# A two-layer graph network on one core: the second layer's first product as seven products of combined quarters

## The chip, the cores and the metric

The kernel runs on one core of a Trainium2 chip. Times are device microseconds of one execution; three runs of the kernel before gave 2491.35, 2492.53 and 2493.94 us, and the profile comes from one further execution. TensorE (PE) multiplies matrices into PSUM; VectorE (DVE), ScalarE (ACT) and GpSimd (POOL) do the elementwise work; SyncE (SP) and POOL issue the transfers. Each engine takes its instructions in the order in which they were written for it.

## The reference

There are 16 graphs of 1024 nodes with 256 channels, in float32. Two layers are added to a residual `x`:

```python
h = jnp.maximum(_layernorm(x, axis=-1), 0.0)
x = x + _L0_gnn_ref(h, L0_gnn_para, adj, L0_gnn_kv_w)      # attention, 4 heads
h = jnp.maximum(_layernorm(x, axis=-1), 0.0)
x = x + _L1_gnn_ref(h, adj, W1, b1, g1, be1, W2, b2, g2, be2)
```

The second layer sums over neighbours and then has two linear maps with batch normalisations:

```python
agg = jnp.einsum('nm,bmd->bnd', A_hat, features)
x = agg.reshape(-1, d)
h = jax.nn.relu(_batchnorm(x @ W1.T + b1, g1, be1))
out = h @ W2.T + b2
out = _batchnorm(out, g2, be2)
```

The case concerns `x @ W1.T + b1`, from 256 to 512 channels, for every node of every graph. The batch normalisation after it needs statistics over all 16 graphs, so its result is written to memory, and the rest of the layer runs when all graphs are done.

## The kernel before, in words

**The stages.** A prologue prepares the neighbour matrix and the first graphs. Then one long loop, `attention`, goes through the graphs. A graph has four units (two pairs of heads, two halves of the nodes), a unit has four steps. Each step issues two score tiles `sc` (L934), two exponentials `p` on ACT (L942), the sums of these on DVE (`acc`, L963 and L966), and the values `o` of the step before (L977). When a unit ends, its sums are folded (L1012, L1013) and added up on PE (`sums`, L1026), and its output goes out and back through memory, is scaled (L1075) and added to `x` (L1083). After the loop, `second` does the last product, the batch normalisations and the output.

**Between the steps** the loop advances a generator, `background(b)`. It weaves three things: for graph b-1, the residual's normalisation (`normed`), the sums over neighbours (`aggregate`) and then the product with W1 (`hidden`); for graph b+2, the preparation of its keys, values and queries (`prepare`): its normalisation, the weighing of the adjacency matrix (`w`, L485 and L493 on ACT, L472 on DVE), squares of its features that are sent through memory to be transposed (`sq`, L412), keys and queries. Every piece yields its estimated PE time, and the loop advances the generator up to a share of `total` that is due at the step (L1109 to L1112). So the order on each engine is written out by the program when it is built; nothing is decided at run time. `soon(...)` puts a small DVE action off to the next piece.

**Sums over neighbours.** `aggregate` is already made of seven products of combined quarters. `made` is one PSUM bank (tile `pa`), and each product is followed by one or two DVE sums out of PSUM into `at`, the result (two tiles, halves of the nodes). A scaling by `dbc` (L706) follows when a quarter is complete.

**The product with W1.** `hidden(b)` makes eight tiles `py` of 128 x 512, one for each half `g` of the nodes and each 128 of the 512 channels, each from two contractions of 128 (L171, the line of the helper that records all such matmuls). ACT adds the bias while it copies a tile to `y` (L773), POOL sends `y` to memory (L774), and DVE takes its statistics (L777). All tiles `pa`, `py`, `sums`, and those of keys, values and queries share the pool `ps_mm` of three PSUM banks, in turn. A matmul into a bank waits until the tile that was there has been read.

**The residual.** `x` of a graph is loaded once into a pool of three places; it serves graph b's first normalisation, then takes the outputs of the attention, is saved (`x_d`, L788) and normalised again. `load_x(b + 3)` follows at the end of `normed(b)`.

The last graph is apart: in `background(15)` its own normalisation, sums over neighbours and product follow those of graph 14 (L1110), and the first products of the last stage are woven in.

Of the kernel before, what the change touches and what calls it, by code (L numbers as in the profile page):

```python
# [10 lines left out]
F32 = mybir.dt.float32  # L11
AF = mybir.ActivationFunctionType
ALU = mybir.AluOpType
# [10 lines left out]
def gnn_two_layers_kernel(  # L24
# [34 lines left out]
    vec = const.tile([P, 18], F32, name="vec")  # L59
    nc.sync.dma_start(out=vec, in_=vecs)  # L60
    b1, g1, be1 = (vec[:, i * HC : (i + 1) * HC] for i in range(3))
    b2, g2, be2 = (vec[:, 3 * HC + i * CC : 3 * HC + (i + 1) * CC] for i in range(3))
    stats1 = const.tile([P, HC, B * NH, 6], F32, name="stats1")
    mv1 = const.tile([P, HC, 2], F32, name="mv1")
# [32 lines left out]
    def layers(shifted):  # L97
# [13 lines left out]
        py = st.enter_context(tc.tile_pool(name=f"py_{kind}", bufs=4))  # L111
# [5 lines left out]
        ps_o = st.enter_context(tc.tile_pool(name=f"ps_o_{kind}", bufs=1, space=PSUM))  # L117
        ps_mm = st.enter_context(tc.tile_pool(name=f"ps_mm_{kind}", bufs=3, space=PSUM))

        xs, hs, hts, ats, qs, ks, vs = {}, {}, {}, {}, {}, {}, {}  # L120
        invs = {}
        csums, cbcs, weighted, weighers = {}, {}, {}, {}
        s1s = {}
        complete = set()

# [2 lines left out]
        def soon(action):  # L128

            queue.append(action)  # L130
# [33 lines left out]
        def bank(name):  # L164
            return ps_mm.tile([P, FB], F32, tag="mm", name=name)
# [4 lines left out]
                r = slice(e * HW, (e + 1) * HW)  # L170
                nc.tensor.matmul(dst[r], left[:, r], right, start=start, stop=stop)  # L171

        def load_x(b):
            xs[b] = p3.tile([P, NT, C], F32, tag="x", name=f"x_{b}")
            parts = 4 if b == 0 else 2
            for part in range(parts):
                t = slice(part * NT // parts, (part + 1) * NT // parts)
                nc.sync.dma_start(
                    out=xs[b][:, t], in_=x[b].rearrange("(t p) c -> p t c", p=P)[:, t]
                )  # L180

        def load_adj(q, th, name):
# [61 lines left out]
        def graph():  # L244
# [21 lines left out]
            for u in range(2 * HT):  # L266
# [20 lines left out]
                nc.gpsimd.dma_start(out=dst[:, 6], in_=one)  # L287
                yield 0.0

        def load_later():  # L290
            later["w1"] = big.tile([P, CC, H1], F32, tag="w1", name="w1")
            nc.sync.dma_start(out=later["w1"], in_=w1_t.rearrange("(k p) j -> p k j", p=P))
            later["dbc"] = const.tile([P, N], F32, tag="dbc", name=f"dbc_{kind}")
            nc.sync.dma_start(out=dinv_d.rearrange("(t p) -> p t", p=P), in_=dinv)
            nc.sync.dma_start(
                out=later["dbc"], in_=dinv_d.rearrange("(o n) -> o n", o=1).to_broadcast([P, N])
            )

        class Norm:
# [2 lines left out]

            def __init__(self, b, first):
                tag = "a" if first else "b"
                self.src = xs[b]
# [376 lines left out]
        def aggregate(b):  # L682


            pieces = []
            order = (0, 2, 5, 1, 4, 6, 3)

            def load(upto):
                while len(pieces) <= min(upto, 7 * NP // 2 - 1):
                    i, th = divmod(len(pieces), NP // 2)  # L690
                    i = order[i]
                    a = p8.tile([P, TH, FB], F32, tag="w", name=f"aht_{b}_{i}_{th}")
                    nc.sync.dma_start(out=a, in_=aht_d[i, th])
                    pieces.append(a)

            load(4)
            yield 0.0
            a11, a12, a21, a22 = quarters("b", b)
            at = ats[b] = [
                p3.tile([P, CC, FB], F32, tag="ht", name=f"at_{b}_{g}") for g in range(NH)  # L700
            ]
            c11, c12, c21, c22 = (at[g][:, c, :] for c in (0, 1) for g in (0, 1))
            add, sub = nc.vector.tensor_add, nc.vector.tensor_sub

            def scale(c, g):
                nc.vector.tensor_mul(c, c, later["dbc"][:, g * FB : (g + 1) * FB])  # L706

            def first(m):
                nc.scalar.copy(c12, m)
                sub(a11, s1s["b", b], a11)  # L710

            def second(m):
                add(c11, m, c12)
                sub(a12, a12, a11)
                soon(lambda: scale(c11, 0))

            def fifth(m):
                add(c22, m, c21)
                add(c12, m, c12)
                soon(lambda: scale(c22, 1))  # L720

            def sixth(m):
                add(c21, m, c21)
                soon(lambda: scale(c21, 0))

            def seventh(m):
                add(c12, m, c12)
                scale(c12, 1)

            for i, (left, after) in enumerate(  # L730
                (
                    (a11, first),
                    (a12, second),
                    (a11, lambda m: add(c12, m, c12)),
                    (a21, lambda m: add(c21, m, c12)),
                    (None, fifth),
                    (a22, sixth),
                    (a12, seventh),
                )
            ):  # L740
                made = bank(f"pa_{b}_{i}")
                left = left or s1s["b", b]
                for th in range(NP // 2):
                    n = i * NP // 2 + th
                    load(n + 5)
                    for j in range(TH):
                        t = th * TH + j
                        product(
                            made, left[:, t, :], pieces[n][:, j, :], t == 0, t == NT // 2 - 1
                        )  # L750
                    if th == NP // 2 - 1:
                        after(made)
                    elif i == 0:
                        combine("b", b, nc.vector)
                    yield 1.71
# [34 lines left out]
        def normed(b):  # L790
            while (b, NH - 1) not in complete:
                yield 0.1
            keep(b)
            yield from Norm(b, False).all()
            if b + 3 < B:
                load_x(b + 3)

        def normed_last():

# [12 lines left out]
        def prepare(b, products):  # L812


            w = weighers[b]
            yield from islice(products, 1)
            if b == 2:
                for k in range(CC):
                    yield from weave(islice(products, 3), (0, islice(w, AHEAD // 3)))
                    yield TOP  # L820
                    transposed(b, (k,))
                    yield 1.0
                yield from products
                return
            squares(b)
            yield from weave(islice(products, 3), (0, islice(w, AHEAD // 2)))
            gathered(b, 0)
            yield from weave(islice(products, 1), (0, islice(w, 1)))
            gathered(b, 1)
            yield from weave(islice(products, 2), (0, islice(w, AHEAD // 2 - 1)))  # L830
            yield from products

        endings, turns = [], []
# [1 line left out]
        def background(b):  # L835

            if b == 0:
# [13 lines left out]
                yield from islice(products, 2)  # L851
                yield from prepare(2, products)
                return
            before = hidden(b - 1)
            gather = aggregate(b - 1)
            if b + 1 < B:
# [236 lines left out]
        def attention():  # L1093
# [7 lines left out]
            for s in range(len(steps) + 2):  # L1101
                if s < len(steps):
                    unit, g = steps[s]
                    b = unit.at[0]
                    if s % per_graph == 0:
# [1 line left out]
                        top = False  # L1107
                        bg, done = background(b), 0.0
                        total = (37.6 if b > 0 else 41.0) * (b + 1 < B) + 24.0 * (b > 0) + 6.0 * (b == 0)  # L1109
                        total += 13.7 * (0 < b < B - 2) + 27.4 * (b == B - 1) + 3.0 * (b == 0)  # L1110

                        total -= 10.3 * (b == B - 1)  # L1112
                    made = scores(*unit.at, g)
# [15 lines left out]
                if before is not None:  # L1129
                    (last, g_last), prs = before  # L1130
                    last.values(g_last, prs)
                    if g_last == NG - 1:
# [29 lines left out]
        with st:  # L1162
# [22 lines left out]
            else:  # L1185
# [24 lines left out]
                load_x(1)  # L1210
                load_x(2)
                run(weave(plain_queries(0), (0, weighers[0]), (5, Norm(1, True).all())))
                attention()
                attn.close()
                turns.append(second(kind))
# [340 lines left out]
```

## Time and profile before

| | us |
|---|---|
| median of three runs | 2492.53 |
| profiled execution | 2492.9 |
| its span | 2491.1 |
| PE busy | 2437.8 (98%) |
| DVE busy | 1880.2 (75%) |
| ACT busy | 1401.8 (56%) |
| POOL busy | 428.0 (17%) |
| matmuls of the product with W1 (1024) | 228.2 |
| matmuls of the sums over neighbours, `pa<-aht,h_b` (1536) | 347.3 |
| scores (4096 matmuls) and values (2048) | 499.5 and 494.5 |

A row of the groups names the source line, the engine, the operation, the tile written and the tiles read, their shapes and the number of instructions; then the busy time and the mean duration in ns; then the idle time of the engine just before these instructions and what ended most of it. A row of the waits has the engine, the tile and line that waited, the one that released it, the total in us, how often, and the longest. A row of the timeline has the start in us, the duration, and the instructions, neighbours of one kind taken together. Matmuls overlap, so the distance from one start to the next says what an instruction costs, and not its duration.

### The profile page before, as it was taken

Reading aid. Unit: us, or ns where it says so; the run is one execution under the profiler, and the core shown is the slowest. Engines: PE = TensorE matmul, PEld = TensorE weight load, DVE = VectorE, ACT = ScalarE, POOL = GpSimd, SP = SyncE. Lnnn points to the kernel's source line nnn. Section 1 sums busy time; section 2 is a strip of 40 time slices with the busy share of each in tenths; the row PEclk is TensorE's granted clock in tenths of the full one; section 3 lists DMA queues with packets and bytes.
Section 4 is the critical chain, followed back from the end, with each engine's and each line's share of the span. In section 5 each row is a group of like instructions: output and inputs, shape, how many; then the busy total and the mean of one; then the engine's idle time right before and its main releaser. Section 6 shows DMA issues by size and latency. Waiting matters only on the chain. (4 is left out here: it accounts for less than half of the span.)

```text
span 2491.1 us, 35563 instructions
## 1 busy us (share of the span) xinstructions
PE 2437.8 (98%) x13403; PEld 842.0 (34%) x13403; DVE 1880.2 (75%) x2919; ACT 1401.8 (56%) x1926; POOL 428.0 (17%) x527
## 2 busy tenths in 40 slices
PE   9999999999999999999999999999999999999995
PEld 4333333333333333333333333333333332334444
DVE  5668787877778787878787787868787876766775
ACT  7775564647474746556464747465564634335544
POOL 1540101010101001010101010110101001036652
PEclk9999999999999999999999999999999999999997
DMA  4754535354544544352635445544536335355459
GB/s 149 238 172 170 172 114 200 98 201 130 194 148 174 168 163 161 125 200 86 214 121 186 141 174 169 178 152 151 171 113 204 103 140 169 123 215 220 189 198 374
DMA packets 187909, 421.42 MB, mean 169 GB/s; under 512 B 21832, under 2 KB 81744, under 8 KB 181968
## 3 DMA queue, kind: packets, MB, share of 16 engines
q1 hardware_dynamic: 158560, 311.56, 37.6%
q0 software_dynamic: 29168, 107.50, 11.6%
q8 instruction: 108, 1.77, 0.3%
q14 instruction: 73, 0.60, 0.1%
HBM read 315.63 MB, written 103.35 MB: 168 GB/s over the span
## 5 line engine op out<-in xcount | busy, mean ns | idle before, releaser
L942 ACT ACTIVATE p<-sc 128x1024 f32<-128x1024 f32 x512 | 494.9, 1019 | 617.4 <-PE sc L934 616.9
L966 DVE TENSOR_TENSOR acc<-acc,p 128x1024 f32<-128x1024 f32 x384 | 472.0, 1229 | 170.3 <-ACT p L942 149.7
L934 PE MATMUL sc<-q,k 64*64 64x512 f32 x4096 | 499.5, 603 | 4.3 <-ACT p L942 4.3
L977 PE MATMUL o<-p,v 128*64 128x512 f32 x2048 | 494.5, 604 | 0.3 <-DVE os L991 0.3
L171 PE MATMUL pg<-w,h_a 128*64 128x512 f32 x1600 | 359.9, 592 | 2.0 <-DVE h_a L558 1.2
L171 PE MATMUL pa<-aht,h_b 128*64 128x512 f32 x1536 | 347.3, 594 | 3.8 <-ACT h_b L342 3.8
L485 ACT ACTIVATE w<-cbc,csum 128x512 f32<-128x512 f32 x256 | 285.9, 1168 | 0.0
L934 PEld LDWEIGHTS sc<-q,k 64*64 64x64 f32 x4096 | 131.0, 132 | 347.6 <-issue 284.1
L171 PE MATMUL py<-at,w 128*64 128x512 f32 x1024 | 228.2, 592 | 0.2 <-ACT y L773 0.2
L472 DVE SCALAR_TENSOR_TENSOR w<-w,adj 128x1024 f32<-128x1024 f32 x128 | 156.2, 1220 | 92.7 <-ACT w L493 88.7
L977 PEld LDWEIGHTS o<-p,v 128*64 128x64 f32 x2048 | 124.4, 136 | 298.3 <-issue 258.6
L995 POOL DMA_DIRECT2D out_d<-os x58 | 34.2, 590 | 1078.5 <-DVE os L991 1044.8
L171 PEld LDWEIGHTS pg<-w,h_a 128*64 128x64 f32 x1600 | 114.9, 137 | 230.5 <-issue 219.4
L171 PEld LDWEIGHTS pa<-aht,h_b 128*64 128x64 f32 x1536 | 110.0, 137 | 218.4 <-issue 202.7
L773 ACT ACTIVATE y<-py,vec 128x512 f32<-128x512 f32 x128 | 87.4, 683 | 114.0 <-PE py L171 89.3
L493 ACT ACTIVATE w<-w 128x1024 f32<-128x1024 f32 x128 | 135.0, 1054 | 1.8
L548 DVE TENSOR_TENSOR w<-w,w 128x1024 f32<-128x1024 f32 x112 | 132.6, 1213 | 1.5
L774 POOL DMA_DIRECT2D y_d<-y x128 | 69.6, 544 | 367.7 <-ACT y L773 358.5
L171 PEld LDWEIGHTS py<-at,w 128*64 128x64 f32 x1024 | 74.1, 137 | 145.5 <-issue 131.2
L171 PE MATMUL pv<-kvw_f,ht 128*64 128x256 f32 x1024 | 116.1, 379 | 0.0
L171 PE MATMUL pk<-ht,kvw_f 128*64 128x512 f32 x512 | 115.2, 592 | 0.2 <-ACT ht L404 0.2
L342 ACT ACTIVATE h_b<-x,lnsm_b 128x256 f32<-128x256 f32 x128 | 69.9, 599 | 66.5 <-DVE lnsm_b L331 66.5
(166 smaller groups left out, 2661.7 us busy)
## 6 DMA issues: line engine op xcount, KB each, us to landing
aht<-aht_d SPq DMA_DIRECT2D x224, 512.0 KB, 6.2
adj<-in_adj_dram SPq DMA_DIRECT2D x128, 512.0 KB, 4.8
y_d<-y POOLq DMA_DIRECT2D x128, 256.0 KB, 3.0
yin_f<-y_d SPq DMA_DIRECT2D x32, 1024.0 KB, 6.5
para<-in_para_dram SPq DMA_DIRECT2D x64, 256.0 KB, 3.3
x_d<-x POOLq DMA_DIRECT2D x16, 1024.0 KB, 5.2
xo_f<-x_d SPq DMA_DIRECT2D x32, 512.0 KB, 8.2
out_dram<-xo_f POOLq DMA_DIRECT2D x32, 512.0 KB, 11.0
```

Source lines behind the costliest of these rows:

```text
L171: nc.tensor.matmul(dst[r], left[:, r], right, start=start, stop=stop)
L342: nc.scalar.activation(self.h[:, t, :], self.src[:, t, :], AF.Relu, bias=self.sm[:, 1, t : t + 1], scale=self.sm[:, 0, t : t + 1], accum_o ...
L472: nc.vector.scalar_tensor_tensor(w, w, 1.0, a, op0=ALU.add, op1=ALU.mult)
L485: nc.scalar.activation(w[:, t, :].rearrange("p (t q) -> p t q", q=P), cbc[:, q * NT // NH : (q + 1) * NT // NH], AF.Abs, bias=csum[:, th * ...
L493: nc.scalar.activation(made[i], made[i], AF.Tanh, scale=-0.5 / C)
L548: nc.vector.tensor_sub(block(i)[part], block(x)[part], block(y)[part])
L773: nc.scalar.activation(y, made, AF.Identity, bias=b1[:, j : j + 1])
L774: nc.gpsimd.dma_start(out=y1_d[i][:, j, :], in_=y)
L934: nc.tensor.matmul(sc[part, e, :], ks[b][k][r, m * P + c * HW : m * P + (c + 1) * HW], qs[b][k][r, f * FB : (f + 1) * FB], start=True, sto ...
L942: nc.scalar.activation(pr, sc, AF.Exp)
L966: nc.vector.tensor_add(self.acc, self.acc, pr)
L977: nc.tensor.matmul(self.o[r, :], vs[b][k][:, m, r], pr[:, e, :], start=(m == 0), stop=(m == NT - 1),)
```

## The change

For graphs 0 to 14 `hidden` is a new function. W1 and the aggregated features are taken as two by two blocks; four combinations `s1` to `s4` of W1 are made once on POOL, and four combinations `t1` to `t4` of the features for each graph (`steps_of`, in which two are on DVE and one on POOL, and `t4` on POOL). Each half `c` of the channel blocks takes seven products, in the order written in the last lines. The eight `y` tiles of a graph are sums of these products, taken on DVE out of PSUM, with two further sums on POOL for each `c`; two tiles are first copied by ACT. For graph 15 the old function stays as `plain_hidden`.

```diff
+        def steps_of(b):
+            b11, b12, _, b22 = at_quarters(b)
+            t1 = p1.tile([P, NT // 2, P], F32, tag="s1", name=f"at1_{b}")
+            t1 = t1.rearrange("p t c -> p (t c)")
+            t2 = p2.tile([P, FB], F32, tag="para", name=f"at2_{b}")
+            nc.vector.tensor_sub(t1, b12, b11)
+            nc.vector.tensor_sub(t2, b22, t1)
+            nc.gpsimd.tensor_sub(b12, b22, b12)
+            steps[b] = t1, t2
...
         def hidden(b):
+            if b == B - 1:
+                yield from plain_hidden(b)
+                return
...
+            nc.gpsimd.tensor_sub(t4, b21, t2)
...
+            def put(y, n, j):
+                i = b * NH + n
+                nc.gpsimd.dma_start(out=y1_d[i][:, j, :], in_=y)
+                soon(lambda: nc.vector.bn_stats(stats1[:, j, i, :], y))
...
+            def m1(c):
+                part = one("1", a11, c, b11)
+                nc.scalar.activation(
+                    new("11", c), part, AF.Identity, bias=b1[:, c : c + 1]
+                )
+            def m2(c):
+                y = made["11"]
+                add(y, one("2", a12, c, b21), y)
+                put(y, 0, c)
+            def m3(c):
+                y = made["12"]
+                add(y, one("3", s4, c, b22), y)
+                put(y, 1, c)
+            def m4(c):
+                y = made["21"]
+                add(y, one("4", a22, c, t4), made["sum"])
+                put(y, 0, 2 + c)
+            def m5(c):
+                nc.scalar.copy(new("22", c), one("5", s1, c, t1))
+                if c == 1:
+                    both(c)
+            def both(c):
+                nc.gpsimd.tensor_add(new("12", c), made["21"], made["22"])
+            def m6(c):
+                y = new("21", c)
+                add(y, one("6", s2, c, t2), made["11"])
+                if c == 0:
+                    both(c)
+            def m7(c):
+                part, y = one("7", s3, c, t3), made["22"]
+                nc.vector.scalar_tensor_tensor(
+                    new("sum", c), part, b1_step[:, c : c + 1], made["21"], op0=ALU.add, op1=ALU.add
+                )
+                nc.gpsimd.tensor_add(y, y, made["sum"])
+                put(y, 1, 2 + c)
+            for c, order in ((0, (m1, m5, m6, m2, m3, m7, m4)), (1, (m1, m6, m2, m5, m7, m3, m4))):
+                for each in order:
+                    each(c)
+                    yield 0.86
```

In the compiled kernel after the change the lines are: the reads of products 2, 3 and 4 L833, L838 and L843, the copy of product 5 L847, the sum with product 6 L856, that with product 7 L862; POOL's two sums L852 and L865; the last sum over neighbours L740.

`x` has two places instead of three, one for the first normalisation and one for the residual, and is read from memory for each:

```diff
-        def load_x(b):
-            xs[b] = p3.tile([P, NT, C], F32, tag="x", name=f"x_{b}")
+        def load_x(b, first=False):
+            into, tag = (firsts, "xn") if first else (xs, "xr")
+            into[b] = p1.tile([P, NT, C], F32, tag=tag, name=f"{tag}_{b}")
...
             yield from Norm(b, False).all()
-            if b + 3 < B:
-                load_x(b + 3)
+            load_x(b + 1)
...
+            if b + 2 < B:
+                load_x(b + 2, True)
             before = hidden(b - 1)
```

The last two sums over neighbours change places, the scaling of the first of them is issued at once, the products are handed to the preparation in other portions, the pool of `y` has six places instead of four, and the pacing follows:

```diff
-            order = (0, 2, 5, 1, 4, 6, 3)
+            order = (0, 2, 5, 1, 4, 3, 6)
...
                 add(c21, m, c21)
-                soon(lambda: scale(c21, 0))
+                scale(c21, 0)
...
+                    (a12, seventh),
                     (a22, sixth),
-                    (a12, seventh),
...
+            yield from islice(products, 1)
             squares(b)
-            yield from weave(islice(products, 3), (0, islice(w, AHEAD // 2)))
+            yield from weave(islice(products, 5), (0, islice(w, AHEAD // 2)))
             gathered(b, 0)
-            yield from weave(islice(products, 1), (0, islice(w, 1)))
+            yield from weave(islice(products, 3), (0, islice(w, 1)))
             gathered(b, 1)
-            yield from weave(islice(products, 2), (0, islice(w, AHEAD // 2 - 1)))
+            yield from weave(islice(products, 3), (0, islice(w, AHEAD // 2 - 1)))
...
-                        total += 13.7 * (0 < b < B - 2) + 27.4 * (b == B - 1) + 3.0 * (b == 0)
+                        total += 12.0 * (0 < b < B - 2) + 25.7 * (b == B - 1) + 3.0 * (b == 0)
...
-                            wait = 5 if last.by_squares and last.at[1:] == (0, 0) else 4
-                            at_mid.setdefault(s + wait - 1, []).append(last.sums)
+                            opens = last.by_squares and last.at[1:] == (0, 0)
+                            wait = 6 if opens else 4
+                            at_mid.setdefault(s + 3 + opens, []).append(last.sums)
```

More of the change, by code (lines that the diff above doesn't have):

```diff
@@ L58, in gnn_two_layers_kernel @@
     nc.gpsimd.memset(neg_half, -0.5)
-    vec = const.tile([P, 18], F32, name="vec")
-    nc.sync.dma_start(out=vec, in_=vecs)
+    vec = const.tile([P, 20], F32, name="vec")
+    nc.sync.dma_start(out=vec[:, :18], in_=vecs)
     b1, g1, be1 = (vec[:, i * HC : (i + 1) * HC] for i in range(3))
+    b1_step = vec[:, 18:20]
+    nc.gpsimd.tensor_sub(b1_step, b1[:, HC // 2 :], b1[:, : HC // 2])
     b2, g2, be2 = (vec[:, 3 * HC + i * CC : 3 * HC + (i + 1) * CC] for i in range(3))
@@ L110, in layers @@
         p8 = st.enter_context(tc.tile_pool(name=f"p8_{kind}", bufs=8))
-        py = st.enter_context(tc.tile_pool(name=f"py_{kind}", bufs=4))
+        py = st.enter_context(tc.tile_pool(name=f"py_{kind}", bufs=6))
         p4 = attn.enter_context(tc.tile_pool(name=f"p4_{kind}", bufs=4, side="right"))
@@ L118, in layers @@
         ps_mm = st.enter_context(tc.tile_pool(name=f"ps_mm_{kind}", bufs=3, space=PSUM))
+        firsts = {}
         xs, hs, hts, ats, qs, ks, vs = {}, {}, {}, {}, {}, {}, {}
         invs = {}
-        csums, cbcs, weighted, weighers = {}, {}, {}, {}
+        csums, cbcs, weighted, weighers, steps = {}, {}, {}, {}, {}
         s1s = {}
@@ L178, in load_x @@
                 nc.sync.dma_start(
-                    out=xs[b][:, t], in_=x[b].rearrange("(t p) c -> p t c", p=P)[:, t]
+                    out=into[b][:, t], in_=x[b].rearrange("(t p) c -> p t c", p=P)[:, t]
                 )
@@ L288, in graph, with w1_quarters @@
                 yield 0.0
+        def w1_quarters():
+            HH = H1 // 2
+            return [later["w1"][:, k, m * HH : (m + 1) * HH] for m in (0, 1) for k in (0, 1)]
         def load_later():
@@ L292, in load_later @@
             nc.sync.dma_start(out=later["w1"], in_=w1_t.rearrange("(k p) j -> p k j", p=P))
+            later["s"] = big.tile([P, 4, H1 // 2], F32, name="w1s")
+            s1, s2, s3, s4 = (later["s"][:, i] for i in range(4))
+            a11, a12, a21, a22 = w1_quarters()
+            nc.gpsimd.tensor_add(s1, a21, a22)
+            nc.gpsimd.tensor_sub(s2, s1, a11)
+            nc.gpsimd.tensor_sub(s3, a11, a21)
+            nc.gpsimd.tensor_sub(s4, a12, s2)
             later["dbc"] = const.tile([P, N], F32, tag="dbc", name=f"dbc_{kind}")
@@ L304, in __init__ @@
                 tag = "a" if first else "b"
-                self.src = xs[b]
+                self.src = firsts[b] if first and b in firsts else xs[b]
                 self.st6 = p1.tile([P, NT, 6], F32, tag="st6", name=f"st6_{tag}_{b}")
@@ L754, in aggregate @@
                         combine("b", b, nc.vector)
+                    elif i == 6 and b < B - 1:
+                        steps_of(b)
                     yield 1.71
-        def hidden(b):
+        def steps_of(b):
[7 more added lines that the diff above has]
+            steps[b] = t1, t2
@@ new lines, in at_quarters, with left, one, new @@
+        def at_quarters(b):
+            return [ats[b][n][:, k] for k in (0, 1) for n in (0, 1)]
+        def hidden(b):
+            if b == B - 1:
+                yield from plain_hidden(b)
+                return
+            HH = H1 // 2
+            a11, a12, _, a22 = w1_quarters()
+            s1, s2, s3, s4 = (later["s"][:, i] for i in range(4))
+            b11, t3, b21, b22 = at_quarters(b)
+            t1, t2 = steps[b]
+            t4 = p2.tile([P, FB], F32, tag="para", name=f"at4_{b}")
+            nc.gpsimd.tensor_sub(t4, b21, t2)
+            def left(block, c):
+                return block[:, c * P : (c + 1) * P]
+            def one(name, block, c, right):
+                part = bank(f"py_{b}_{c}_{name}")
+                product(part, left(block, c), right, True, True)
+                return part
+            made = {}
+            def new(name, c):
+                made[name] = py.tile([P, FB], F32, tag="y", name=f"y_{b}_{c}_{name}")
+                return made[name]
+            def put(y, n, j):
+                i = b * NH + n
+                nc.gpsimd.dma_start(out=y1_d[i][:, j, :], in_=y)
+                soon(lambda: nc.vector.bn_stats(stats1[:, j, i, :], y))
+            add = nc.vector.tensor_add
+            def m1(c):
[37 more added lines that the diff above has]
+                    yield 0.86
@@ L759, in hidden, with plain_hidden @@
+        def plain_hidden(b):
             at = ats[b]
@@ L1209, in layers @@
                 run(weave(products, (0, islice(weighers[0], AHEAD))))
-                load_x(1)
-                load_x(2)
+                load_x(1, True)
                 run(weave(plain_queries(0), (0, weighers[0]), (5, Norm(1, True).all())))
+                load_x(2, True)
                 attention()
```

## The prediction

> **What bounds the kernel now.** I read the totals first, then the 40 slices, the costliest groups, the waits of PE and DVE, and last the timelines of one graph's turn at this product.
>
> ```profile
> PE 2437.8 (98%) x13403; PEld 842.0 (34%) x13403; DVE 1880.2 (75%) x2919; ACT 1401.8 (56%) x1926; POOL 428.0 (17%) x527
> PE   9999999999999999999999999999999999999995
> PEclk9999999999999999999999999999999999999997
> L171 PE MATMUL py<-at,w 128*64 128x512 f32 x1024 | 228.2, 592 | 0.2 <-ACT y L773 0.2
> L773 ACT ACTIVATE y<-py,vec 128x512 f32<-128x512 f32 x128 | 87.4, 683 | 114.0 <-PE py L171 89.3
> ```
>
> PE is busy 98% of the span at full clock, and the product concerned (tiles py) waits 0.2 us in the whole run. Its 1024 instructions are 64 per graph; ACT alone reads their PSUM tiles. PE sets the time here, so its work counts fully, provided that the tiles are still read in time. The longest waits of PE and of DVE:
>
> ```profile
> PE sc L934 <- ACT p L942: 4.3, 7, 1.1
> PE pa L171 <- ACT h_b L342: 3.8, 2, 2.8
> ```
>
> ```profile
> DVE acc L966 <- ACT p L942: 149.7, 94, 4.3
> DVE w L472 <- ACT w L493: 88.7, 35, 7.9
> ```
>
> DVE's 25% idle is waiting for ACT, not lack of work in a ready queue. The timeline of PE and then of DVE in one turn (start, us, instruction):
>
> ```profile
> 826.76 5.32 PE L171 MATMUL py<-at,w 128*64 128x512 f32 x24
> 832.01 1.95 PE L934 MATMUL sc<-q,k 64*64 64x512 f32 x16
> 833.89 1.94 PE L977 MATMUL o<-p,v 128*64 128x512 f32 x8
> 835.66 5.32 PE L171 MATMUL py<-at,w 128*64 128x512 f32 x24
> ```
>
> ```profile
> 824.57 0.70 DVE L1012 STREAM_TRANSPOSE acc<-acc 128x512 f32<-128x512 f32 x1
> 825.31 0.69 DVE L1013 TENSOR_REDUCE part<-acc 128x16 f32<-128x512 f32 x1
> 825.91 2.54 DVE L966 TENSOR_TENSOR acc<-acc,p 128x1024 f32<-128x1024 f32 x2
> 828.37 2.37 DVE L412 STREAM_TRANSPOSE sq<-h_a 128x1024 f32<-128x1024 f32 x2
> 830.66 1.25 DVE L777 BATCH_NORM_STATS2 stats<-y 128x6 f32<-128x512 f32 x2
> ...
> 838.27 1.22 DVE L472 SCALAR_TENSOR_TENSOR w<-w,adj 128x1024 f32<-128x1024 f32 x1
> 839.41 1.28 DVE L777 BATCH_NORM_STATS2 stats<-y 128x6 f32<-128x512 f32 x2
> ```
>
> Start to start gives what I use below: 24 matmuls 5.25 us (0.88 for 4), a step's scores 1.88, its values 1.77; on DVE a fold 0.74+0.60, two accumulations 2.46, the two square transposes 2.29, the weighing multiply 1.14, one statistics instruction 0.58.
>
> [...] L966 takes 1410 ns where it overlaps POOL tensor work against 1218 elsewhere. [...] in the trace PE's 2.76 us gap at 2097.68 is followed by slow matmuls (8 in 3.03 us, usually 1.89), its gaps of 1.64 and 1.48 us at 2222.30 and 2227.70 are not.
>
> **The change part by part.** *Matmuls.* Graphs 0 to 14: fourteen half-size products of 4 instructions, 56 for 64. Eight instructions are 1.75 us (15 x 1.75 = 26 us if nothing else happens).
>
> *Readers.* Per graph 8 ACT passes (683 ns) become 4; DVE takes over 10 sums from PSUM (0.61 each, as L706's and L735's start-to-start; the one with a bias step 0.75, from L1374's 750 ns), plus t1 and t2 (2 x 0.61): 7.6 us more on DVE, some 114 us in all, on an engine with 611 us idle. POOL gets six 128x512 operations, by interpolation between 0.73 us (256 columns, unhindered) and 2.36 (1024) about 1.27 each: 7.6 us on an engine 83% idle. Neither is a bound by total. What matters is where a DVE sum is what frees one of the three rotating banks.
>
> *The ledger of a turn*, from A, the start of the last sum of the aggregation (L740 after); PE then is 0.17 us into the first product. Before A, DVE has some 6.2 us of work (a sum, a scale, t1, t2, fold, two accumulations) in PE's 7.2, so A is still set by PE. PE's order: products 1, 5, 6, 2 | scores, values | 3, 7, 4 and the second half's 1 | second half's 6. It would start the last at A - 0.17 + 4x0.88 + 1.88 + 1.77 + 4x0.88 = A+10.5. That product takes the bank of the first half's product 7, free when L862 has read it. DVE's order up to there: L740 0.72, scale 0.61, squares 2.29, L856 0.71, L833 0.61, fold 1.34: A+6.28. Its accumulation waits for an exponential: ACT does y 0.58, copy 0.6, two weighings 2.25 and their tanh 0.95 first, and then the exponential 1.0, done by about A+6.6. Two accumulations 2.46: A+9.1; L838 0.61; weighing multiply 1.14; statistics 0.58; L862 0.75: **A+12.2**. PE stalls 12.2 - 10.5 = **1.7 us**, as much as the turn saves. It is no drain that a later slack can repay: PE is in order, and scores, values and the rest queue behind it; ACT's exponentials come later with them. Bounds: 1.1 us if ACT is early (-0.3) and the sums of PSUM pipeline as plain ones (-0.3); 2.3 if an accumulation meets a POOL operation (+0.2) and ACT's weighing is behind (+0.4). I take 1.7, and 0.2 more for the second half, where product 3 finds its bank freed (L833) only some 0.15 us ahead of need and statistics wait for a POOL sum. Per graph -1.75 + 1.9 = about +0.2; for graphs 0 to 12, 13 x 0.2 = +2.5 us.
>
> *DVE leaves the turn 2 to 3 us later.* What is next there is the wait of the weighing multiply for ACT (3.7 us in the keys' stage), which absorbs it.
>
> *Graph 14* runs with the last normalisation, where DVE is the limit: counted from the end of its aggregation, the third product of graph 15 starts after 31.1 us instead of 29.25: +1.9 instead of -1.75.
>
> *Graph 13* is woven with graph 14's normalisation, which already stalls PE 2.76 us at 2097.68 and costs the clock. The 1.75 us saved ahead of it is given up in that wait, while DVE sums and POOL sums and DMA issues (0.54 each) now stand before its statistics and reciprocal roots: +1 to +3, taken as +2.
>
> *x.* Two single places; each half-graph load is issued again, 15 MB more on 421, or 6 us of 16 queues at the mean rate spread over 2490. Reads land in 5.3 us; the residual's, issued at 781 after the normalisation, lands at 786, and its first use, 790.2 before, is put a step later, about 797. Cost nothing; without that cover 1 to 2 us per graph. SP's queue waits for the same readers as before. *Order of the last two sums, the immediate scale, products spread 1/5/3/3, later first add, pacing totals 12.0 and 25.7:* these place work; priced inside the ledger. The transposed queries' input is released later, landing about A+23.2 for a need at A+25.3: 2 us slack where there were 8, nothing. *Once:* four POOL differences of weights (4 x about 0.7 us) and a bias step, under the prologue: nothing.
>
> Sum: +2.5 + 1.9 + 2 = +6.4. The profiled execution took 2492.9 (span 2491.1), within the runs' 2491.35 to 2493.94; on it 2499.3, on the median about 2499.
>
> **Rivals.** *A, likeliest (0.5): the bank wait eats the saving*, 2488 to 2507, at 2499. For it: three banks, in-order DVE, the ledger. Against: it rests on terms of 0.3 us each, times 13.
>
> *B (0.27): the stall is short or absent, faster.* If DVE's pieces run ahead in most turns (the accumulation not held by ACT, or work ahead of L862 already done), the stall falls to 0.6: 13 x (0.8 - 1.75) = -12, with +4 at the end: 2484. Without any stall 13 x -1.75 + 4: 2474; with the last two graphs gaining too, 2466. It decides once the stall is below 1.75 - 0.3, that is 1.4 us with nothing added after. For it: DVE has 25% idle; against: that idle lies at ACT's waits.
>
> *C (0.23): slower by PE's clock.* If stalls of 1.7 us, with the scores' later waits, bring the half clock that the 2.76 us gap brought, each costs 1.1 us in 8 matmuls and about 0.7 in the next 8: 13 x 1.8 = 23, 2522; in half the turns 2511. It decides somewhere between 1.64 (seen harmless) and 2.76 us. A late transposed input of queries (landing up to 5.8 us for 3.8 uses up the 2 us) would come out likewise.
>
> **How the numbers follow.** The measurement tells 0.2%, 5 us, from no change: 2487.5 to 2497.5. A gives 0.04 faster, 0.2 same, 0.26 slower; B 0.27 faster; C 0.23 slower: 0.31, 0.20, 0.49. The range leaves the full gain below and the full clock loss above: 2472 to 2518; A's own is 2488 to 2507.
>
> **What would show it.** Right: a matmul count of py of 15 x 56 + 64 = 904; PE gaps of 1.1 to 2.3 us, once a graph, before the second half's product 6, released by DVE's L862; DVE near 1990 us busy, ACT about 40 us less; PE's busy time 20 us less and its idle time 25 more. Wrong: no such gap (B); slow matmuls after it or a lower clock in the slices (C); gaps elsewhere, at queries, keys or the residual's x, would mean a mechanism that I've priced at nothing.

## The result and the profile after

The changed kernel takes 2514.61 us (median of four runs, 2514.51 to 2515.03) against 2491.94 before (four runs, 2491.34 to 2493.94): 1.0089 of it, 95% interval 1.0077 to 1.0101. It is slower by 22.7 us, inside the range of the prediction (2472 to 2518) and on the side given the larger chance, but 15.6 us above the predicted 2499.

The page of the changed kernel: totals, PE's slices and its granted clock, and the rows of the product with W1. The columns are those of the page before.

```profile
span 2512.8 us, 35881 instructions
...
PE 2420.4 (96%) x13283; PEld 830.0 (33%) x13283; DVE 1998.0 (80%) x3099; ACT 1369.4 (54%) x1866; POOL 555.3 (22%) x622
...
PE   9999999999999999999999999999999997999995
PEclk9999999999999999999999999999999999999997
...
L174 PE MATMUL py<-at,w1s 128*64 128x512 f32 x480 | 114.5, 597 | 18.0 <-DVE y_sum L862 18.0
L174 PE MATMUL py<-at,w 128*64 128x512 f32 x424 | 108.2, 601 | 4.3 <-DVE y L833 1.1
```

PE has 120 matmuls less (13283 against 13403, 8 for each of 15 graphs) and is busy 17.4 us less, yet the span grew by 21.7: PE now idles 39 us more. One slice near the end has fallen to 7. The view of PE's waits (total, times, longest) names most of it:

```profile
PE pa L174 <- DMA aht<-aht_d: 18.0, 1, 18.0
PE py L174 <- DVE y_sum L862: 18.0, 14, 1.3
...
PE sums L1144 <- DVE y L843: 1.8, 1, 1.8
...
PE py L174 <- DVE y L833: 1.1, 1, 1.1
```

There are two waits of 18 us of very different kinds: 14 for DVE's read of product 7 (1.31 us in each of the graphs 0 to 12, 1.03 in the tail), and a single one for a transfer of the neighbour matrix.

To see where the time goes I cut both traces at the first score matmul of each graph. A graph's turn is the time from one such start to the next; the last turn ends with the last score matmul, the tail with PE's last instruction. A steady turn is one of graphs 3 to 13 (of 4 to 13 where work is put ahead of product 7, at the end of the experiments), which agree within 0.03 us. These numbers, in us, are worked out from the starts of the instructions in the traces (the last score matmul and PE's last instruction are taken at their end):

```
                         start    turns 0-14     of these,   turn of    tail    last PE
                                   together       steady     graph 15           instruction
before                   55.58     2002.95        135.96     102.57    299.61   2460.71
after                    54.88     2005.31        136.10     116.41    305.80   2482.40
difference               -0.70       +2.36         +0.14     +13.84     +6.19    +21.69
```

("Turns 0-14 together" runs from the first score of graph 0 to that of graph 15.) So the steady turns hardly moved, and 20.0 of the 21.7 us are in the last two stretches: the turn of graph 15, in which graph 13's product and graph 14's normalisation and sums are placed, and the tail, which begins in graph 14's product.

**A steady turn.** DVE's timeline in one turn of the changed kernel (start, us, instruction, and in brackets the idle time before it):

```profile
1099.59 0.69 DVE L740 TENSOR_TENSOR at<-pa,at 128x512 f32<-128x512 f32 x1 [0.50 <-PE pa L174]
...
1106.19 2.56 DVE L1084 TENSOR_TENSOR acc<-acc,p 128x1024 f32<-128x1024 f32 x2 [0.19 <-ACT p L1060]
1108.66 0.68 DVE L838 TENSOR_TENSOR y<-py,y 128x512 f32<-128x512 f32 x1
1109.26 1.22 DVE L489 SCALAR_TENSOR_TENSOR w<-w,adj 128x1024 f32<-128x1024 f32 x1
1110.40 0.69 DVE L821 BATCH_NORM_STATS2 stats<-y 128x6 f32<-128x512 f32 x1
1111.00 0.73 DVE L862 SCALAR_TENSOR_TENSOR y_sum<-py,vec,y 128x512 f32<-128x512 f32 x1
```

and PE's in the same turn (product 1 of the second half is the later four of the eight `py<-at,w` at 1108.27, its product 6 the four at 1111.79):

```profile
1106.56 1.89 PE L174 MATMUL py<-at,w1s 128*64 128x512 f32 x8
1108.27 2.21 PE L174 MATMUL py<-at,w 128*64 128x512 f32 x8
1111.79 1.08 PE L174 MATMUL py<-at,w1s 128*64 128x512 f32 x4 [1.31 <-DVE y_sum L862]
1112.80 1.95 PE L1052 MATMUL sc<-q,k 64*64 64x512 f32 x16
```

The prediction's ledger, counted from L740's start at A = 1099.59, can be held against it: L862 ends at A+12.1 (predicted A+12.2); the matmuls of product 6 start at A+12.2, where they could have come at about A+10.4 (predicted A+10.5). From start to start of the matmuls, the second half's products 1 and 6 lose 0.27 + 0.05 + 1.48 + 0.05 = 1.85 us to banks; eight matmuls fewer save 1.72. The remainder, +0.13, is the measured +0.14 almost to the digit.

**The turn of graph 15.** SP's queue, before and then after (start and duration of the issues, the line, the transfer, how many):

```profile
2091.58 2.74 SPq L1001 DMA_DIRECT2D os<-out_d  x4
2094.42 19.84 SPq L693 DMA_DIRECT2D aht<-aht_d  x6
```

```profile
2105.97 0.95 SPq L183 DMA_DIRECT2D xr<-in_x_dram  x2
2107.02 3.40 SPq L710 DMA_DIRECT2D aht<-aht_d  x7
2111.59 4.06 SPq L1119 DMA_DIRECT2D os<-out_d  x4
```

Before, the pieces of the neighbour matrix for graph 14 are asked for from 2094.42 on. After, two loads of x stand ahead of them and are issued only at 2105.97. That is the moment at which ACT has made the last normalised rows of graph 14, as ACT's timeline shows:

```profile
2096.75 2.08 ACT L359 ACTIVATE h_b<-xr,lnsm_b 128x256 f32<-128x256 f32 x4 [2.61 <-DVE lnsm_b L348]
2103.88 2.07 ACT L359 ACTIVATE h_b<-xr,lnsm_b 128x256 f32<-128x256 f32 x4 [5.05 <-DVE lnsm_b L348]
```

The residual's x has one place now, so x of graph 15 can't be loaded before graph 14's x is normalised, and the neighbour pieces behind it in the queue can't be asked for either. On PE:

```profile
2112.91 6.42 PE L174 MATMUL pa<-aht,h_b 128*64 128x512 f32 x16 [18.05 <-DMA aht<-aht_d]
```

18.05 us of wait, and then 16 matmuls in 6.42 us that take 3.60 otherwise: the granted clock was 0.61 from 2094 to 2112 and 0.59 from 2112 to 2120.

### The profile page after: what moved, and what is told of

Same layout as the page of the kernel before. It is cut to its first block, busy times and chain, and to the rows that moved or that the text cites. A ratio compares the mean times of both kernels' runs of the same rounds, so it can differ in the third digit from the quotient of the medians.

```text
span 2512.8 us, 35881 instructions
## 1 busy us (share of the span) xinstructions
PE 2420.4 (96%) x13283; PEld 830.0 (33%) x13283; DVE 1998.0 (80%) x3099; ACT 1369.4 (54%) x1866; POOL 555.3 (22%) x622
## 5 line engine op out<-in xcount | busy, mean ns | idle before, releaser
L174 PE MATMUL py<-at,w1s 128*64 128x512 f32 x480 | 114.5, 597 | 18.0 <-DVE y_sum L862 18.0
L174 PE MATMUL py<-at,w 128*64 128x512 f32 x424 | 108.2, 601 | 4.3 <-DVE y L833 1.1
L359 ACT ACTIVATE h_a<-xn,lnsm_a 128x256 f32<-128x256 f32 x120 | 70.6, 594 | 74.7 <-DVE lnsm_a L348 74.7
L1081 DVE TENSOR_TENSOR acc<-p,p 128x1024 f32<-128x1024 f32 x64 | 78.9, 1233 | 31.0 <-ACT p L1060 31.0
L1422 ACT ACTIVATE yin_f<-yin_f,sm_f 128x512 f32<-128x512 f32 x128 | 93.6, 803 | 16.6 <-DMA yin_f<-y_d 13.7
```

Source lines behind the costliest of these rows:

```text
L1081: nc.vector.tensor_add(self.acc, self.held, pr)
L1422: nc.scalar.activation(y, y, AF.Relu, bias=sh[:, j : j + 1], scale=scale[:, j : j + 1])
```

## The experiments

Theory: three separate waits on PE's path. In the steady turns, the bank that DVE's read of product 7 frees; in graph 15's turn, the load of x 15 that holds up SP's queue; in the tail, banks again, in graph 14's product. Rivals: the product's extra DVE and POOL work delays graph 14's normalisation; the second reading of x, or the DVE work as such, lengthens the turns; the waits only cover one another.

**x 15 behind the neighbour pieces.**

```diff
-            load_x(b + 1)
+            if b < B - 2:
+                load_x(b + 1)
...
                 yield from weave(endings.pop(), (2, normed(b - 1)))
                 yield next(gather)
+                load_x(b)
```

> The changed kernel with one load moved: the residual's x of graph 15 is issued on SP behind the first neighbour-matrix loads of graph 14 instead of in front of them. Theory (SP's queue: that load waits for graph 14's last normalised rows, and the neighbour pieces queue behind it): PE's wait of 18.05 us at graph 14's first sum over neighbours falls to 2 to 4 us, for the normalised rows, and the slow matmuls after it get fewer; the last turn of the loop falls from 116.4 to about 101 to 103 us; median 2514.6 - 16 = about 2498.5 (2496 to 2501). Rival (the extra DVE and POOL work of graph 13's product delays the normalisation): the wait stays at 15 to 18, median 2512 to 2515.

Measured: 2497.48 us (2496.83 to 2499.02; 1.0023 of before, 1.0014 to 1.0032), 17.1 less than the changed kernel. The turn of graph 15 is 99.14 us. PE's wait at graph 14's first sum is now for the normalised rows, and the matmuls after it are at full speed:

```profile
2096.47 3.65 PE L174 MATMUL pa<-aht,h_b 128*64 128x512 f32 x16 [2.55 <-ACT h_b L359]
```

So the order on SP's queue was the cause of 17 us. With it out of the way the turn of graph 15 is 3.4 us *shorter* than before (102.57), but only a part of that is the gain of the seven products. The turn holds 12 matmuls of `py` fewer (60 for 72, 2.6 us): eight are saved, and four of graph 14's product now fall behind the last score, into the tail. About 1.7 us more is my estimate for the clock, half of 3.41: the profiled execution of before shows a granted clock of 0.50 from 2098.38 to 2101.79, this one 1.00 throughout the turn. Against that stands a new wait of 0.87 us for an exponential.

**The plain product for all graphs, the rest of the change kept.**

```diff
-            if b == B - 1:
+            if True:
                 yield from plain_hidden(b)
...
-                    elif i == 6 and b < B - 1:
+                    elif False:
                         steps_of(b)
```

with pacing and portions as before.

> The changed kernel with the plain product for all graphs, its pacing and portions as before; the two places of x, the doubled reads, the swapped sums and the later first add stay. Theory: steady turns go back to 135.96 us (they are 136.10 with the seven products), the wait of about 18 us at graph 14's sums stays (15 to 20), graph 14's own product is as before; median 2491.9 + 16 = about 2508 (2505 to 2512). Rival (the product's own DVE and POOL work made that wait): the wait falls to about 3 us, median 2491 to 2494. Rival (the x traffic makes the steady turns longer): turns stay at 136.1.

Measured: 2504.85 us (1.0051, 1.0034 to 1.0068), some 12 above before and just below the range that was expected. Every steady turn is 135.96 us, as before to the hundredth: reading x twice, the swapped sums and the later first add cost nothing there. The wait stays, without the seven products:

```profile
PE pa L174 <- DMA aht<-aht_d: 14.6, 1, 14.6
```

The two runs together settle it: the wait comes from the places of x and the order on the queue. It is 14.6 us without the seven products and 18.05 with them, so some 3.5 us of it come with the product. ACT's timelines show how: its two groups of normalised rows of graph 14 start 3.3 us apart here (2095.46 and 2098.76), as before, and 7.1 us apart in the changed kernel, where DVE, kept back by the sums of graph 13's product, takes a fold and two accumulations between them (2097.24 to 2101.03) and not ahead of both. The rival that the product delays the normalisation is thus right for a fifth of the wait.

**Products 3 and 7 as one piece.**

```diff
                 for each in order:
                     each(c)
-                    yield 0.86
+                    if c == 0 and each is m3:
+                        continue
+                    yield 1.72 if c == 0 and each is m7 else 0.86
```

and one piece less in the first portion of products, so that the portions hold the same work.

> The changed kernel with products 3 and 7 of the first half issued as one piece, so that DVE reads product 7 straight after product 3, ahead of the weighing multiply and one statistics instruction. Theory (PE waits for the bank of product 7): the 1.31 us wait before the second half's product 6 goes, about 0.3 before its product 1 stays; steady turns 136.10 - 1.5 = 134.6 us (134.4 to 134.9), 13 x 1.5 = 19 us less, median about 2495.5 (2492 to 2499). Rival (the bank's wait only hides another limit of DVE or ACT): a wait of similar length elsewhere in the turn, steady turns 135.8 to 136.1, median 2511 to 2515.

Measured: 2504.09 us (1.0048, 1.0031 to 1.0064), 10.5 less than the changed kernel, where 19 was expected. The steady turns are 135.39 (expected 134.6). The wait for product 7 is gone, and a smaller one has come up, for the bank of product 2 in the second half (L833):

```profile
PE py L174 <- DVE y L833: 7.8, 13, 0.6
```

The DVE timeline shows why: the read L833 stands behind two accumulations.

```profile
1104.09 0.74 DVE L862 SCALAR_TENSOR_TENSOR y_sum<-py,vec,y 128x512 f32<-128x512 f32 x1
...
1110.06 2.49 DVE L1086 TENSOR_TENSOR acc<-acc,p 128x1024 f32<-128x1024 f32 x2
1112.47 0.68 DVE L833 TENSOR_TENSOR y<-py,y 128x512 f32<-128x512 f32 x1
```

PE comes earlier to this place now, so the slack is used up. The mechanism held and its size was off by this second wait.

**Both edits.**

> Both edits together: the load of x 15 behind the neighbour pieces, and products 3 and 7 as one piece. Theory (two separate waits on PE's path, so the gains add): 2514.6 - 16 - 19 = about 2479.5 (2476 to 2484), below the kernel before (2491.9). Rival (one of them moves into the other): 2493 to 2499.

Measured: 2487.43 us (0.9982, 0.9974 to 0.9989). It is 27.2 less than the changed kernel; the two alone gave 17.1 and 10.5. They add, so they are separate waits. The number lies above the range that was expected (2476 to 2484), because the second edit alone brought less.

**The plain product for graph 14 too.** As the last kernel, with the condition `b >= B - 2` for the plain product.

> x 15 behind the neighbour pieces, products 3 and 7 as one piece, and the plain product for graph 14 as well as 15. Theory (in graph 14's product the DVE reads stand among the sums and the normalisation of graph 15, and PE waits for banks there): the time from the end of the loop's scores to the last PE instruction falls from 306.4 us to about 299.6, as in the kernel before; median 2487.4 - 6.5 = about 2481 (2479 to 2484). Rival (graph 15's normalisation limits that stretch whatever the product): 2486 to 2489.

Measured: 2483.80 us (0.9969, 0.9957 to 0.9980), 3.6 less. The tail is 300.70 us, against 299.61 before and 306.39 with the seven products in graph 14. So the product of graph 14 makes the long tail, in part by the clock: with the seven products the granted clock is 0.50 there from 2164.26 to 2171.09, which by my estimate can cost 2.5 us (half of the 5.09 that PE is busy in it), and with the plain one nowhere in this stretch. The 1.1 us that remain above the kernel before are left open. And the turn of graph 15 grew by 1.7 us (99.20 to 100.93), as the product's beginning lies in it, so that the gain is 3.6 and not 6.5. The rival's 2486 to 2489 is excluded.

In the tail of the changed kernel, in graph 14's product, PE goes from one bank to the next like this:

```profile
2186.43 1.08 PE L174 MATMUL py<-at,w 128*64 128x512 f32 x4 [1.10 <-DVE y L833]
2187.81 1.08 PE L174 MATMUL py<-at,w 128*64 128x512 f32 x4 [0.30 <-DVE y L838]
2189.91 1.08 PE L174 MATMUL py<-at,w1s 128*64 128x512 f32 x4 [1.03 <-DVE y_sum L862]
2192.79 0.31 PE L1144 MATMUL sums<-part,same 128*64 128x32 f32 x4 [1.80 <-DVE y L843]
2193.29 0.85 PE L1172 MATMUL ot<-ident,os 128*128 128x128 f32 x4 [0.19 <-ACT y L827]
2194.57 1.97 PE L174 MATMUL py<-at,w 128*64 128x512 f32 x4 [0.43 <-DVE y L856]
```

Together 4.85 us, and the last four matmuls take 1.97 us where 1.03 is usual.

**Product 5 ahead of product 2 in the second half.** As the last kernel, and in the line that gives the order (only its second half is shown):

```diff
-(1, (m1, m6, m2, m5, m7, m3, m4))
+(1, (m1, m6, m5, m2, m7, m3, m4))
```

Product 5 is read by ACT, and product 3 now takes its bank.

> As the kernel with the three edits, and in the second half product 5 (read by ACT) ahead of product 2 (read by DVE). Theory (the 0.6 us wait left in each turn is product 3 waiting for DVE's read of product 2, behind two accumulations): that wait goes, steady turns 135.39 - 0.7 = 134.7 us (134.3 to 134.9), 12 x 0.7 = 8 us less than with three edits, median about 2473 (2470 to 2477). Rival (DVE is late all over the turn, so the wait moves to product 4 or to the keys): steady turns 135.2 to 135.5, 2479 to 2483.

Measured: 2472.06 us (2472.01 to 2472.61; 0.9923, 0.9906 to 0.9939), faster than both kernels: 19.9 less than before, 42.6 less than the changed one. The steady turns are 134.57, which is 1.39 less than before; of the 1.72 that eight matmuls take, 0.33 are still lost, the 0.27 ahead of the second half's product 1 among them. Its page:

```profile
PE 2413.8 (98%) x13291; PEld 829.3 (34%) x13291; DVE 1990.1 (81%) x3087; ACT 1372.8 (56%) x1870; POOL 565.5 (23%) x616
```

DVE and POOL have nearly the same busy time as in the changed kernel, with all the sums of the seven products for graphs 0 to 13. For these graphs the work was not the trouble, only its order.

**One statistics instruction more ahead of the read of product 7.** To see whether PE follows that read, I put DVE work in front of it (in `m7`, for the first half): first a whole statistics instruction.

```diff
                 part, y = one("7", s3, c, t3), made["22"]
+                if c == 0:
+                    nc.vector.bn_stats(stats1[:, 0, b * NH, :], made["11"])
```

> The changed kernel with one statistics instruction (0.58 us, start to start) taken twice on DVE ahead of the read of product 7 in the first half. Theory (PE waits for DVE's read of that bank, and DVE is busy without a break from its wait for an exponential to that read): the wait before the second half's product 6 grows from 1.31 to about 1.9 us, steady turns from 136.10 to 136.7. Rival (DVE has slack there, the bank is freed by something else): steady turns stay at 136.1.

Measured, one execution: 2519.71 us, steady turns 136.48, not 136.7. The waits were other ones:

```profile
PE py L174 <- ACT y L827: 10.2, 13, 0.8
PE py L174 <- DVE y L833: 10.0, 14, 1.1
```

Product 6 waited for ACT's read of product 1. In the compiled program the bank had changed: product 6 got another of the three. So the banks don't simply take turns, as the description of the kernel has it; by what rule the pool hands them out, no run shows. The experiment had changed two things. Two smaller amounts take them apart: over 64 columns, where the compiled program keeps the bank, and over 128, where it is swapped (into a slot that is overwritten later).

```diff
+                if c == 0:
+                    nc.vector.bn_stats(stats1[:, 0, (b + 1) * NH, :], made["12"][:, :64])
```

> The changed kernel with a statistics instruction over 64 columns ahead of DVE's read of product 7 in the first half; in the compiled program the second half's product 6 still waits for that read. From 0.58 us for 512 columns and 0.33 for 256 (start to start) it costs about 0.14 us. Theory (PE waits for that read): the wait grows from 1.31 to about 1.45 us, steady turns from 136.10 to 136.24. Rival (the read isn't what sets the wait): 136.10.

> The same over 128 columns, about 0.21 us; in the compiled program the second half's product 6 now has another bank, that of product 1, which ACT reads. Theory (only the wait for the bank counts): the wait is 0.8 us, as where a whole statistics instruction was added and the bank was changed too, and the later wait for DVE's read of product 2 is some 0.4 to 0.5 us shorter than there (0.69): steady turns 135.9 to 136.2, so that more DVE work costs nothing or less than nothing. Rival (DVE's work as such lengthens the turn): 136.3 or more.

Measured, one execution each: 2516.07 and 2511.59 us. With the bank kept, the wait is

```profile
PE py L174 <- DVE y_sum L864: 19.8, 14, 1.4
```

and the steady turns 136.22 to 136.23, 0.13 longer for an instruction that takes 0.13 us on DVE (1111.22 to the next start at 1111.35): PE follows that read one for one here. With the bank swapped the turns are 135.94, 0.16 *shorter* than in the changed kernel, with more DVE work in each. What the turn cost in these runs was set by which read frees which bank, and not by how much DVE had to do.

## Why the prediction was right or wrong

The prediction added 2.5 us in the turns, 2 in graph 13's part and 1.9 in graph 14's, 6.4 in all. Measured were 2.36 in turns 0 to 14, 13.84 in the turn of graph 15 and 6.19 in the tail, less 0.70 at the start.

*Matmuls and busy times: right.* 904 matmuls of py (480 + 424) as predicted, DVE 1998.0 us busy (near 1990), ACT 32 less (predicted 40), PE 17.4 less (20), POOL 127 more (114; its 128x512 sums, estimated at 1.27 us, took 1.28 to 1.35 on average and 1.71 for the one of `steps_of`). PE's idle time grew by 39 us, where 25 was forecast. One reading was only half right: of DVE's 611 us idle before, its waits put about 287 down to ACT and 236 to PE, so that it was not waiting for ACT alone. And in the kernel before, the accumulations that meet POOL's work took 1449 ns on average (18 of them, from 1214 to 2565), not 1410, against 1218 for the others.

*The ledger of a steady turn: right.* The stall was forecast at 1.7 us for the bank that L862 frees, 1.31 was shown as one wait and 1.85 was lost to banks in all; the turn was forecast at +0.2 and came to +0.14. The further remark that product 3 in the second half has only 0.15 us of slack named the wait that came up in the experiment. That stalls of this kind are avoidable without any work taken away (134.57 us) the prediction didn't ask.

*x at nothing: wrong, and this is the step that failed.* "SP's queue waits for the same readers as before" holds for graphs 0 to 12. There the first five neighbour pieces are issued ahead of the load of x, as in this turn of the changed kernel:

```profile
1045.76 2.26 SPq L710 DMA_DIRECT2D aht<-aht_d  x5
1053.10 0.94 SPq L183 DMA_DIRECT2D xr<-in_x_dram  x2
```

For graph 14 it doesn't hold: before, `load_x(b + 3)` isn't issued there at all, since b + 3 is past the last graph; after, `load_x(b + 1)` is, for graph 15, and the normalisation is finished before the first neighbour piece is asked for. So a load with a late wait was put ahead of loads that PE needs next. I looked at the regular turn and not at the last one. It cost 17.1 us with the clock that fell after it. Among its signs of being wrong the prediction had named gaps elsewhere, from a mechanism priced at nothing, and this is one.

*Graph 13 at +2: wrong in sign, right in part of its mechanism.* The delay of the normalisation that was forecast is there, with the load moved too: ACT's two groups of rows start 7.1 us apart (2095.82 and 2102.94) for 3.3 before. But PE's first sum starts at 2096.47, ahead of the second group. Its wait is 2.55 us for 2.76, and of the delay no more than the wait of 0.87 us reaches PE. Without the clock and the four matmuls that moved, the turn is some 0.9 us shorter than before, about half of what eight matmuls take.

*Graph 14 at +1.9: right in kind, too small.* The tail grew by 6.2 us. I counted DVE's chain to graph 15's rows and left out that PE waits at six places on the way, 4.85 us, with a lower clock (0.89 from 2184 to 2200). Plain products there bring the tail back to 300.7.

*The rivals.* A, the bank wait eating the saving, is what happened in the steady turns. B needed a stall under 1.4 us in all and didn't occur. C's time (2511 to 2522) was met, but not by its mechanism: thirteen stalls of 1.31 us in the turns brought no slow matmuls (the granted clock was 1.00 from 0 to 2090 us), and its 0.7 us for the matmuls behind the first 8 was 0.54 in the trace of before (16 scores in 2.42 us from start to start, usually 1.88). Up to the end of graph 14's product the clock was lower only about the 18 us and in the tail (0.61 from 2094 to 2112, 0.59 from 2112 to 2120, 0.89 from 2184 to 2200). So it is luck that the result lies in the range: A's own ended at 2507, the part above was there for C's clock loss, and what filled it was the load of x, which had been priced at nothing. C also looked for a length of wait, between 1.64 and 2.76 us, at which the clock falls; that there is one, these runs don't show (last section).

## What to carry to other kernels

Where PE set the time, fewer matmuls paid only as far as their banks were read in time (turns of 136.10 and 134.57 us with the same matmuls, 135.96 with eight more): write down for each bank which instruction frees it and what stands ahead of that instruction on its engine, and reorder until those reads come first. When a buffer loses places, look at every queue that its loads stand in, and above all at the last rounds, where a guard used to drop the load and other loads follow directly. An edit that changes durations can also change which bank a tile gets, as one statistics instruction did here (product 6 then waited 0.8 us for L827 and not 1.31 for L862); compare the compiled waits before reading a small experiment. And before a microsecond or two between two traces is put down to a change, see whether both executions lost the same clock.

## What was not expected of the hardware

With the load of x moved, a single PE wait of 2.55 us left the matmuls at full speed (16 in 3.65 us; the granted clock was 1.00 from 2092.03 to 2098.86), while before one of 2.76 us had been followed by 8 in 3.03, usually 1.89. In the changed kernel six waits, together 4.85 us and none above 1.80, lie between 2184 and 2200 us, where the granted clock was 0.89; the kernel before has a wait of 1.64 us at 2222.30, and from 2218 to 2226 its clock was 1.00. So in these traces the length of one wait doesn't tell whether the clock falls.

The first stretch below is the kernel before at the wait of 2.76 us; the others are the changed kernel at the wait of 18.05 us and at the six. A row has the stretch, its length, the busy time and number of instructions of PE and then of the other engines, and in the third place from the end the granted clock.

```profile
2097.00:2102.00 5.00, 4.32 (x16) 1.13 (x20) 1.79 (x7) 3.76 (x8) 1.25 (x2) 0.66 0.88 244
...
2094.00:2112.00 18.00, 0.86 (x5) 0.00 (x0) 9.23 (x22) 4.29 (x9) 4.08 (x7) 0.61 0.54 189
2112.00:2120.00 8.00, 7.09 (x24) 2.27 (x28) 0.63 (x2) 0.59 (x1) 0.00 (x0) 0.59 1.02 401
2184.00:2200.00 16.00, 11.16 (x48) 2.98 (x44) 15.47 (x40) 3.24 (x6) 6.79 (x10) 0.89 0.23 83
```

Why the clock fell after one of these waits and not after another, the runs don't show.

Also, the wait ahead of product 6 cost more than the trace names: 1.48 us from start to start for a wait of 1.31. A matmul of that product is shown with 0.59 us, while the next pair usually starts 0.43 us after it, and the wait is counted from the end.
